# A conv-attention-scan network with a sorted mixture of experts: table numbers written earlier, two independent result adds, another spacing of expert tiles

## The chip, the cores and the metric

One Trainium2 chip, one of its cores. The metric is the device time of one execution in microseconds. The core has five engines with a queue each: TensorE (PE), VectorE (DVE), ScalarE (ACT), GpSimd (POOL) and SyncE (SP), which here only issues transfers. POOL and ACT issue transfers too[...].

## The reference, cut to what matters

```python
x = x + conv_block(_ln_c(x))          # 4 images of 256 channels, 32 x 32 points
t = _to_tokens(x)                     # 4 * 1024 tokens of 256
t = t + ffn(_ln_t(t))
def ffn(xf):                          # 8 experts, 2 of them for each token
    top_w, top_i = top_k(xf @ Wg + bg, 2);  top_w = softmax(top_w)
    for e in range(8):
        h = gelu(xf @ W1[e] + b1[e])  # 256 -> 1024
        out = out + w_dense[:, e:e+1] * (h @ W2[e] + b2[e])
```
`conv_block` is a layer norm, four selective scans of 64 channels each (state of 16), gates and short convolutions, attention with 8 heads beside a local convolution, a product of both with a norm and a gelu, a 3 x 3 convolution by channel, a norm and a last product.

## The kernel before

All of it is one program in float32. The Python code is a set of generators, each of which issues a part of the network and yields a number of ticks until it wants to be called again; `beat()` calls those whose tick has come. The order in which they are called is the order in each engine's queue, and nothing is moved afterwards.

**The front, by images.** The selective scan of an image has 4 x 2 parts of 16 steps. In a step ACT makes the decay `dA`, DVE the increment and the scan `hs` (lines 538, 545), POOL multiplies `hs` by the spread row `cs` (line 550), PE sums (line 556). Beside the scan of image b, `convolutions(b-1)`, `attention(b-1)`, `joined(b-1)`, `around(b-2)` and `sent_off(b-2)` run. `around` has the 3 x 3 taps on DVE: two chunks of channels, eight `scalar_tensor_tensor` each (line 1040). `sent_off` has the last norm (`mean`, squares `sq_fin`, `var_fin`, `r_fin`), the last product (`pr`) and `experts.dispatch`.

**Routing.** `dispatch(b)` turns the image into rows of tokens (transposes `raw`), stores them in `Y`, makes the gate's product, picks two experts for each token, and counts with two products `places` (lines 1499, 1500) where each row goes in a long array `XS` of one region per expert. `count` and `counted` are then known. It writes the rows with 16 indirect transfers from POOL (line 1560), a memset of a one-column tile `apart` ahead of each (line 1559), with a yield after each. At the last image, `blank_ends` first writes blank rows behind each region's end: ACT loads eight addresses from `ends_i` and issues eight transfers (line 1380).

**Tiles.** The expert part works on 39 tiles of 256 rows of one expert each: a first series of 8 after image 1 has been routed, a second of 8 after image 2, a third of 23 after image 3. `tiles()` issues 35 of them in order; the last 4 of the third series lie behind branches in `run` and are executed only if the number of tiles asks for them. A series starts with its table: `series` calls `tiles_of` and `table`, which write two number patterns with POOL's iota (`steps`, line 1582, and `which`, line 1603) and compute from them and the counts, in some 20 short DVE instructions, which expert and which row each tile has. `load` fetches a tile's weights, `rows` its 256 rows of `XS` (line 1709), both with an address that SP loads from the table. `front` transposes the rows (`xp`, line 1755, to `xT`, line 1756). `tile` makes the hidden rows (line 1778), gelu on ACT in pairs (line 1783), and the second product (line 1788); DVE adds a bias and weights the result `ys` (lines 1793, 1798), and two indirect transfers add it into `Y`, one for each half of 128 rows (line 1799). The second of them waits until the first has landed. A tile yields after each of its eight pieces, and while tile n is issued, `ahead(n + 1)` loads the next: its load in the first piece, rows in the second, front from the sixth on.

**Spacing.** After image 3's scan `convolutions(3)` is issued with `around(2)`, `sent_off(2)` and tiles, then `attention(3)` alone, then `joined(3)`, `around(3)`, `sent_off(3)` in one chain beside the tiles. In this chain `pace(b, ticks)` sets how many ticks a piece of a tile yields: the larger, the fewer pieces between two steps of the chain. The last tile of the second series is held until the rows of image 3 are sent.

At the end `bring_back` loads `Y` (line 1810), transposes it (line 1819) and stores it.

Of the kernel before, what the change touches and what calls it, by code (L numbers as in the profile page):

```python
# [9 lines left out]
F32 = mybir.dt.float32  # L10
# [4 lines left out]
P = 128  # L15
C = 256
# [6 lines left out]
NE, DFF = 8, 1024  # L23
# [48 lines left out]
def network(  # L72
# [70 lines left out]
    with tc.tile_pool(name="w_conv", bufs=1) as wp, tc.tile_pool(  # L143
# [902 lines left out]
        def sent_off(b):  # L1046

            xc = XC.pop(b)

            def centre(h, mean):  # L1050
                for c in range(NC2):
                    nc.vector.tensor_tensor(
                        xc[:, c, half(h)], xc[:, c, half(h)], mean, ALU.subtract
                    )

            pace(b, PACE["norm"])
            xr = a8(f"xr_{b}")
            nc.sync.dma_start(xr, x[b].rearrange("(c p) n -> p c n", p=P))
            yield from in_turn(
                range(2),  # L1060
                lambda h: column_mean(f"mean_{b}_{h}", [xc[:, c, half(h)] for c in range(NC2)]),
                centre,
            )
            yield from inverse_deviation(f"fin_{b}", xc)

            def residual(at, r):
                co, h = at
                inner = xr[:, co, half(h)]
                nc.vector.scalar_tensor_tensor(
                    inner, r, prb[:, co : co + 1], inner, ALU.add, ALU.add  # L1070
                )

            yield from in_turn(
                CO_H, lambda at: product(
                    f"pr_{b}_{at[0]}_{at[1]}", projT_s, at[0],
                    [xc[:, ci, half(at[1])] for ci in range(NC2)],
                ), residual,
            )
            pace(b, PACE["rows"])
            yield from experts.dispatch(  # L1080
                b, xr, act8.tile(experts.XR, F32, tag="a8", name=f"XR_{b}"), root,
                log_exp,
            )
            T["sent", b] = True
            pace(b, 1)


        def tiles():
# [3 lines left out]
            order = order[: len(order) - LATE]  # L1092
            got, xs, tables = {}, {}, experts.tables

            def known(n):
                return experts.counted >= B - 3 + order[n][0]

# [3 lines left out]
            def load(n):  # L1101
                s, i = order[n]
                if i == 0:
                    tables.append(experts.series(
                        s, lambda name, shape: act2.tile(shape, F32, tag="a2", name=name)
                    ))
                if n == 0:
                    w1 = [a8("w1_0")[:, :, 0:DFF]]
                    w2 = [a8("w2_0").rearrange("p c (k x) -> p (c k) x", x=C)]
                else:  # L1110
                    w = [
                        acts.tile([P, N], F32, tag="dts", name=f"w_{n}_{k}") for k in range(3)
                    ] + [actd.tile([P, N], F32, tag="dt", name=f"w_{n}_3")]
                    w1, w2 = w[0:2], [v.rearrange("p (k c) -> p k c", c=C) for v in w[2:4]]
                b2_s = actc.tile([P, C], F32, tag="cs", name=f"b2_{n}") if n else a2("b2_0")[:, 0:C]
                got[n] = experts.load(s, i, tables[s], w1, w2, b2_s)
# [22 lines left out]
            for n in range(len(order)):  # L1139
                while n not in got or len(got[n]) == 4:  # L1140
                    ahead(n, NHC)
                    yield 4

                while n == sum(experts.SERIES[:2]) - 1 and not sent(n + 1):
                    ahead(n + 1, 0)
                    yield 1
                while not T.get(("scanned",)):
                    yield 1
                while T.get(("hold",)):
# [58 lines left out]

        PARTS = 2 * NB

        PACE = {"product": 3, "norm": 1.7, "taps": 0.67, "rows": 1.6}
        with tc.manual_schedule(engines=ALL):
            log_exp()
            start(normalised(0), weights())
# [73 lines left out]
class Experts:  # L1288
# [7 lines left out]

    T = 256

    SERIES = (8, 8, 23)
# [4 lines left out]
    def __init__(self, ctx, tc, psum, B, b1, ident, eps5, ones_mean, Wg, bg, W1, W2, b2, out):  # L1306
# [10 lines left out]
            tc.tile_pool(name="moe_dram", bufs=1, space=bass.MemoryType.DRAM)  # L1317
        )
        self.XS = md.tile([self.SPARE + T, self.ROW], F32, name="XS")
        self.Y = md.tile([NTOK + P, C], F32, name="Y")  # L1320
        m0 = self.m0 = ctx.enter_context(tc.tile_pool(name="moe0", bufs=1))

        blank = self.blank = m0.tile([P, self.ROW], F32, name="blank")
        nc.gpsimd.memset(blank, 0.0)
        nc.gpsimd.iota(
            blank[:, C : C + 1], [[0, 1]], base=NTOK, channel_multiplier=1,
            allow_small_or_imprecise_dtypes=True,
        )
        nc.gpsimd.memset(blank[:, C + 3 : C + 4], -1.0)
        nc.scalar.dma_start(self.Y[ds(NTOK, P), :], blank[:, 0:C])  # L1330

        Wg_s = m0.tile([P, NC2, NE], F32, name="Wg_s")
        nc.gpsimd.dma_start(Wg_s, Wg)
# [38 lines left out]
        self.sent, self.sent_by = [], []  # L1372
        self.tables = []
        self.counted = -1
        self.read = []
        self.blank_rows(self.SPARE)

    def blank_rows(self, at):

        ins = self.nc.scalar.dma_start(  # L1380
            self.XS[ds(at, self.T), :].rearrange("(n p) c -> p n c", p=P),
            self.blank.rearrange("p (a c) -> p a c", a=1)
            .to_broadcast([P, self.T // P, self.ROW]),
        )
        for other in self.sent + self.read:
            self.tc.declare_no_dep(ins.ins, other.ins, reason="no two share a row")
        self.sent.append(ins)
# [47 lines left out]
    def dispatch(self, b, X1, XR, root, log_exp):  # L1435
# [117 lines left out]
        if b == self.B - 1:  # L1553
            self.blank_ends()

        apart = m0.tile([P, 1], F32, tag="apart", name=f"apart_{b}")
        for j in range(2):
            for t in range(NT):
                nc.gpsimd.memset(apart, 0.0)
# [15 lines left out]
        for other in others:  # L1575
            self.tc.add_manual_dep(ins.ins, other.ins.name, kind, reason=reason)

    def tiles_of(self, temp, name, rows, base=0):

        nc, K = self.nc, self.NTOK // self.T  # L1580
        steps = temp(f"steps_{name}", [P, NE, K])
        nc.gpsimd.iota(
            steps, [[0, NE], [self.T, K]], base=base, channel_multiplier=0,
            allow_small_or_imprecise_dtypes=True,
        )
        nc.vector.tensor_tensor(steps, rows.to_broadcast([P, NE, K]), steps, ALU.is_gt)
        ntile = temp(f"ntile_{name}", [P, 1, NE])
        nc.vector.tensor_reduce(ntile.rearrange("p a e -> p e a"), steps, AX.X, ALU.add)
        return ntile

    def table(self, temp, keep, name, n, ntile, done=None):


        nc = self.nc
# [4 lines left out]
        starts = temp(f"starts_{name}", [P, 1, NE])  # L1599
        nc.vector.tensor_tensor(starts, ends, ntile, ALU.subtract)  # L1600
        S = [P, n, NE]
        which, past = temp(f"which_{name}", S), temp(f"past_{name}", S)
        nc.gpsimd.iota(
            which, [[1, n], [0, NE]], base=0, channel_multiplier=0,
            allow_small_or_imprecise_dtypes=True,
        )
        nc.vector.tensor_tensor(past, which, ends.to_broadcast(S), ALU.is_ge)
        inside = temp(f"inside_{name}", S)
        nc.vector.tensor_tensor(inside, which, starts.to_broadcast(S), ALU.is_ge)
# [25 lines left out]
    def series(self, s, temp):  # L1635
# [7 lines left out]
            assert before + n == self.NTILE  # L1643
        else:
            assert (before + n) * T <= 2 * N * b - NE * (T - 1)
        ntile = self.tiles_of(temp, s, self.count[:, :, b : b + 1], 0 if last else T - 1)
        if s:
            nc.vector.tensor_tensor(ntile, ntile, self.done, ALU.subtract)
        table, starts, ends = self.table(temp, self.kept, s, n, ntile, self.done if s else None)
        if last:  # L1650
            self.used = self.m0.tile([P, 1], mybir.dt.int32, name="used")
            nc.vector.tensor_copy(self.used, ends[:, :, NE - 1 : NE].rearrange("p a e -> p (a e)"))
# [116 lines left out]
    def tile(self, j, got, hs, ys):  # L1769
# [26 lines left out]
        )  # L1796
        for t in range(2):
            nc.vector.tensor_scalar(ys[:, t, :], ys[:, t, :], wgt[:, t, :], None, ALU.mult)  # L1798
            nc.gpsimd.indirect_dma_start(  # L1799
                out=self.Y[:, :],  # L1800
                out_offset=bass.IndirectOffsetOnAxis(ap=dest[:, t, :], axis=0),
                in_=ys[:, t, :], in_offset=None, compute_op=ALU.add,
            )

    def bring_back(self, b, m2):

# [120 lines left out]
```

## Time and profile before

| | |
|---|---|
| time, median of 3 (lowest to highest) | 2480.68 us (2478.96 to 2487.04) |
| profiled execution: span, mean PE clock granted | 2485.2 us, 0.913 |
| busy, of the span: PE, DVE, ACT, POOL | 85%, 65%, 48%, 45% |
| scan of image 3 ends (last `hs` on POOL) | about 1684 us |
| attention of image 3 on PE | 1893 to 1964 us |
| `places` of image 3 | 2105.5 us |
| front of tile 16 | 2167.15 us |
| last product of the last tile ends | about 2444.5 us |

The profile's times run from the first instruction. A line of the timeline gives start, length, engine, line of the code, operation, what is written and read, and in brackets how long the engine stood idle before it and which instruction or transfer ended that. `SPq` and `ACTq` are the queues from which these engines issue transfers. One matrix product of the code makes two matmul records in float32. Ends of matmuls are modelled, and a few records can be missing.

### The profile page before, as it was taken

The page shows a single profiled execution, that of the slowest core. Times are in us where ns is not written, and L with a number is a line of the kernel's source. Part 1 is how long each engine was busy: PE and PEld are TensorE (multiplying, and loading weights), DVE is VectorE, ACT ScalarE, POOL GpSimd, SP SyncE. Part 2 cuts the span into 40 slices and gives each one's busy share as a digit, 9 for nine tenths or more (in the row PEclk, how much of TensorE's full clock was granted, in tenths as well). Part 3 has the DMA queues.
Part 4 walks back from the last instruction along what each step waited for, and adds up shares of the span by engine and source line. Part 5 has one row for each costly group of instructions (what it writes and reads, how often), then busy time and mean ns, then how long its engine had stood idle before and what let it go on. Part 6 is the DMA issues. An engine that isn't in the chain of part 4 may idle for free. (4 is left out here: it accounts for less than half of the span.)

```text
span 2485.2 us, 28288 instructions
## 1 busy us (share of the span) xinstructions
PE 2122.3 (85%) x8810; PEld 941.7 (38%) x8810; DVE 1622.3 (65%) x2243; ACT 1193.9 (48%) x2016; POOL 1111.8 (45%) x1163
## 2 busy tenths in 40 slices
PE   5776778899977799998589999758999999599995
PEld 2121112333311132232013223204773477588884
DVE  2688998876799887789978877985424354111211
ACT  1544455368663647765253686413427654122221
POOL 2577777541577661176775405562112011322221
PEclk8799997899998889997788999868999999899997
DMA  3443342220243321033333202334431154566664
GB/s 95 99 109 93 96 117 70 72 70 27 51 103 97 75 61 34 28 105 98 97 80 77 57 18 51 90 100 145 115 112 36 55 154 142 176 195 196 190 195 148
DMA packets 154541, 244.17 MB, mean 98 GB/s; under 512 B 34017, under 2 KB 103301, under 8 KB 154377
## 3 DMA queue, kind: packets, MB, share of 16 engines
q1 hardware_dynamic: 133856, 215.46, 30.7%
q0 software_dynamic: 13744, 19.31, 3.8%
q10 hardware_dynamic: 6776, 7.45, 0.9%
q8 instruction: 74, 1.21, 0.2%
q14 instruction: 91, 0.74, 0.1%
HBM read 141.16 MB, written 33.85 MB: 70 GB/s over the span
## 5 line engine op out<-in xcount | busy, mean ns | idle before, releaser
L550 POOL TENSOR_TENSOR hs<-hs,cs 128x512 f32<-128x512 f32 x512 | 669.5, 1309 | 222.0 <-DVE hs L545 175.1
L556 PE MATMUL yp<-hs,quads 128*32 128x512 f32 x1024 | 344.5, 684 | 173.1 <-POOL hs L550 123.2
L531 ACT ACTIVATE dA<-dts,A 128x512 f32<-128x512 f32 x512 | 342.9, 713 | 291.6 <-DMA dts<-dt 185.7
L538 DVE TENSOR_TENSOR dBu<-dts,bs 128x512 f32<-128x512 f32 x512 | 348.1, 680 | 80.5 <-DMA dts<-dt 24.2
L545 DVE TENSOR_TENSOR_SCAN hs<-dA,last,dBu 128x512 f32<-128x512 f32 x256 | 327.7, 1280 | 24.9 <-DVE dBu L538 0.5
L1799 POOL DMA_INDIRECT Y<-ys,dest x70 | 112.6, 1609 | 512.7 <-DVE ys L1798 362.2
L545 DVE TENSOR_TENSOR_SCAN hs<-dA,dBu 128x512 f32<-128x512 f32 x256 | 312.5, 1221 | 30.6 <-ACT dA L531 5.7
L1783 ACT ACTIVATE hs<-h,b 128x256 f32<-128x256 f32 x280 | 117.0, 471 | 405.5 <-PE h L1778 265.6
L871 ACT ACTIVATE e<-st 128x512 f32<-128x512 f32 x512 | 263.1, 606 | 87.2 <-PE st L861 86.7
L1788 PE MATMUL y<-w,hs 128*128 128x256 f32 x1120 | 259.6, 383 | 4.8 <-ACT hs L1783 4.8
L1778 PE MATMUL h<-xT,w 128*128 128x256 f32 x1120 | 253.2, 382 | 0.8 <-DVE xT L1756 0.8
L1788 PEld LDWEIGHTS y<-w,hs 128*128 128x128 f32 x1120 | 212.2, 192 | 43.4 <-issue 10.1
L1778 PEld LDWEIGHTS h<-xT,w 128*128 128x128 f32 x1120 | 213.3, 191 | 40.2 <-issue 9.7
L1756 DVE COPY xT<-xp 128x512 f32<-128x512 f32 x35 | 24.2, 692 | 297.8 <-PE xp L1755 297.8
L556 PEld LDWEIGHTS yp<-hs,quads 128*32 128x32 f32 x1024 | 55.6, 117 | 429.0 <-POOL hs L550 287.4
L523 PE MATMUL bs<-u,xpwT_s 128*32 128x512 f32 x1024 | 176.9, 670 | 40.6 <-DVE hs L545 23.6
L549 POOL COPY last<-hs 128x1 f32<-128x1 f32 x256 | 66.3, 259 | 318.0 <-DVE hs L545 309.5
L913 DVE TENSOR_TENSOR e<-e,e 128x512 f32<-128x512 f32 x256 | 171.4, 732 | 53.9 <-PE av L903 44.0
L861 PE MATMUL st<-qk 32*128 32x512 f32 x1024 | 194.0, 655 | 6.8 <-DVE hs L545 4.5
L439 PE MATMUL up<-xn,inwk 64*128 64x512 f32 x256 | 131.7, 659 | 15.6 <-DVE hs L545 9.2
L903 PE MATMUL av<-e,v 128*32 128x512 f32 x1024 | 142.7, 621 | 0.0
L861 PEld LDWEIGHTS st<-qk 32*128 32x128 f32 x1024 | 68.1, 188 | 132.4 <-issue 88.1
(271 smaller groups left out, 2499.3 us busy)
## 6 DMA issues: line engine op xcount, KB each, us to landing
w<-in_W_dram SPq DMA_DIRECT2D x136, 512.0 KB, 4.0
dts<-dt SPq DMA_DIRECT2D x512, 128.0 KB, 2.4
cs<-cd SPq DMA_DIRECT2D x512, 64.0 KB, 2.0
xs<-XS SPq DMA_DIRECT2D x35, 260.0 KB, 4.5
b<-in_b_dram SPq DMA_DIRECT2D x35, 128.0 KB, 4.2
xn<-in_x_dram SPq DMA_DIRECT2D x4, 1024.0 KB, 5.7
XL<-xl SPq DMA_DIRECT2D x8, 512.0 KB, 2.8
xl<-XL SPq DMA_DIRECT2D x4, 1024.0 KB
```

Source lines behind the costliest of these rows:

```text
L523: nc.tensor.matmul(bs[r], xpwT_s[:, n, s : s + 1].to_broadcast([P, 32]), T[b, n, "u"][:, half(h)], start=True, stop=True,)
L531: nc.scalar.activation(dA, T[b, n, h, "dts", g][:, 0, :], AF.Exp, scale=A[:, g, n, q : q + 1])
L538: nc.vector.tensor_tensor(dBu, T[b, n, h, "dts", g][:, 1, :], T[b, n, h, "bs", q], ALU.mult)
L545: nc.vector.tensor_tensor_scan(hs, T[b, n, h, "dA", i], dBu, 0.0 if h == 0 else last, ALU.mult, ALU.add)
L550: nc.gpsimd.tensor_tensor(hs, hs, T[b, n, h, "cs", q], ALU.mult)
L556: nc.tensor.matmul(T[b, n, h, "yp"][ts(g, 32)], quads, T[b, n, h, "hs", q * GD + g], start=(q == 0), stop=(q == GS - 1),)
L861: nc.tensor.matmul(sts[i], k[r, ts(kt, P)], q[r, half(h)], start=True, stop=not shifted)
L871: nc.scalar.activation(es[i], sts[i], AF.Exp, scale=1.0 / HD**0.5)
L903: nc.tensor.matmul(accs[0][ts(i, HD)], v8[:, kt, ts(4 * g + i, HD)], es[i], start=(kt == 0), stop=(kt == NK - 1),)
L913: nc.vector.tensor_tensor(first[i], first[i], es[i], ALU.add)
L1778: nc.tensor.matmul(hp[:, i, :], w1(c, k), xT[:, c, :], start=(c == 0), stop=(c == NC2 - 1))
L1788: nc.tensor.matmul(yp[:, ts(t, C)], hs[:, k, ts(t, P)], w2(k), start=(k == 0), stop=(k == NHC - 1))
```

## The change

1. **Number patterns.** A new function `count_up(s)` writes `steps` and `which` of series s. It is called for series 0 when `tiles()` starts, five ticks ahead of the rest, and for series 1 and 2 when tile 2 and tile 10 (the third of their series) start. `tiles_of` and `table` take the patterns instead of writing them.
2. **Adds.** The two adds of a tile are declared to be independent, with a memset of `apart` between them; each waits for both adds of the tile before. The rows of a blank tile get 256 different numbers instead of twice the same 128, for which `Y` and the tile `blank` grow. `apart` is one tile for the whole kernel.
3. **Spacing.** In the chain of image 3 a piece of a tile yields 4 ticks instead of 3 at the products, 2.2 instead of 1.7 at the norms, 0.9 instead of 0.67 at the taps, and in `dispatch` 2 until the counts are known and 0.75 after it instead of 1.6. The hold of the second series' last tile is removed.

```diff
-            pace(b, PACE["rows"])
-            yield from experts.dispatch(
+            pace(b, PACE["routing"])
+            for ticks in experts.dispatch(
                 b, xr, act8.tile(experts.XR, F32, tag="a8", name=f"XR_{b}"), root,
                 log_exp,
-            )
+            ):
+                if experts.counted == b:
+                    pace(b, PACE["rows"])
+                yield ticks
...
+            experts.count_up(0, temp)
+            yield 5
...
-                while n == sum(experts.SERIES[:2]) - 1 and not sent(n + 1):
-                    ahead(n + 1, 0)
-                    yield 1
+                if order[n] in ((0, 2), (1, 2)):
+                    experts.count_up(order[n][0] + 1, temp)
...
-        PACE = {"product": 3, "norm": 1.7, "taps": 0.67, "rows": 1.6}
+        PACE = {"product": 4, "norm": 2.2, "taps": 0.9, "routing": 2, "rows": 0.75}
...
-        self.Y = md.tile([NTOK + P, C], F32, name="Y")
+        self.Y = md.tile([NTOK + T, C], F32, name="Y")
...
+    def count_up(self, s, temp):
+        nc, K, n = self.nc, self.NTOK // self.T, self.SERIES[s]
+        steps = temp(f"steps_{s}", [P, NE, K])
+        nc.gpsimd.iota(steps, ...)
+        which = temp(f"which_{s}", [P, n, NE])
+        nc.gpsimd.iota(which, ...)
+        self.numbers[s] = steps, which
...
-            nc.gpsimd.indirect_dma_start(
+        added = []
+        for t in range(2):
+            if t:
+                nc.gpsimd.memset(self.apart, 0.0)
+            ins = nc.gpsimd.indirect_dma_start(
                 out=self.Y[:, :],
                 out_offset=bass.IndirectOffsetOnAxis(ap=dest[:, t, :], axis=0),
                 in_=ys[:, t, :], in_offset=None, compute_op=ALU.add,
             )
+            for other in added:
+                self.tc.declare_no_dep(ins.ins, other.ins, reason="no two share a row")
+            self.follow(ins, self.added, "a row may be added to by both")
+            added.append(ins)
+        self.added = added
```

## The prediction

> **What bounds the kernel now.** The chain of waits on the page starts at 2476.48 and says nothing here, so I read in this order: TensorE (PE) busy time by stage, who PE waits for, then the queue of each engine at the places found. All times are of the profiled execution (span 2485.2 us; the three timed runs gave 2478.96 to 2487.04, median 2480.68). I sum differences and put them on the median.
>
> Busy time by stage, from the end of image 3's attention (1964) on: length, busy us with record counts for PE, PE weight loads, DVE, ACT, POOL, then granted clock, DMA share, GB/s.
> ```profile
> 2001.00:2044.00 43.00, 40.32 (x187) 34.44 (x187) 30.88 (x44) 25.41 (x39) 9.82 (x5) 1.00 0.67 200
> 2044.00:2086.00 42.00, 37.05 (x145) 26.15 (x144) 13.06 (x28) 14.23 (x23) 6.19 (x4) 1.00 0.41 117
> 2086.00:2106.00 20.00, 19.93 (x119) 17.73 (x118) 10.74 (x44) 8.87 (x18) 3.10 (x2) 1.00 0.63 178
> 2106.00:2135.00 29.00, 26.17 (x126) 22.73 (x126) 10.17 (x42) 7.71 (x16) 14.76 (x23) 1.00 0.77 224
> 2135.00:2168.00 33.00, 10.60 (x50) 9.09 (x49) 5.31 (x22) 3.36 (x8) 11.23 (x17) 0.71 0.47 147
> 2168.00:2445.00 277.00, 276.62 (x1308) 242.84 (x1306) 48.68 (x153) 63.81 (x152) 58.61 (x38) 0.99 0.62 178
> ```
> Length minus PE busy is the idle: 2.7, 4.9, 0.1, 2.8, 22.4, 0.4 us. From 2168 PE is full and nothing but PE work counts; the 22.4 us is one wait. PE's waits from 1690 on (waiting line, releaser, total us, times, longest):
> ```profile
> PE xp L1755 <- DMA xs<-XS: 22.4, 1, 22.4
> PE op L1819 <- DMA yy<-Y: 19.6, 4, 16.2
> PE var_fin L343 <- ACT sq_fin L949: 6.5, 2, 3.7
> ```
> Tile 16, the first that needs the last routing, waits for its rows. Why so late is in POOL's queue (start, length, what, idle before it and its releaser):
> ```profile
> 1642.48 0.30 POOL L1582 IOTA steps<- 128x128 f32 x1
> ...
> 1649.13 1.27 POOL L550 TENSOR_TENSOR hs<-hs,cs 128x512 f32<-128x512 f32 x1 [6.18 <-DVE hs L545]
> ...
> 2144.04 1.61 POOL L1799 DMA_INDIRECT Y<-ys,dest  x1 [0.30 <-issue]
> 2148.62 1.56 POOL L1799 DMA_INDIRECT Y<-ys,dest  x1 [2.97 <-issue]
> 2149.63 0.86 POOL L1582 IOTA steps<- 128x128 f32 x1
> ```
> and in DVE's and ACT's:
> ```profile
> 2150.53 0.29 DVE L1586 TENSOR_TENSOR steps<-count,steps 128x128 f32<-128x128 f32 x1 [14.75 <-POOL steps L1582]
> ```
> ```profile
> 2115.94 10.27 ACTq L1380 DMA_DIRECT2D XS<-blank  x8
> 2126.26 3.03 ACT L1783 ACTIVATE hs<-h,b 128x256 f32<-128x256 f32 x8 [15.52 <-DMA XS<-blank]
> ```
> Line 1582 and line 1603 write the number patterns of a table. The third table's stood behind 16 row transfers and two scatter-adds; DVE idled 14.75 us for them. ACT could issue no gelu for 11.3 us (2114.99, end of ends_i, to 2126.26), held by eight address loads. The tail:
> ```profile
> 2445.90 1.54 POOL L1799 DMA_INDIRECT Y<-ys,dest  x1 [7.79 <-DVE ys L1798]
> 2450.47 1.54 POOL L1799 DMA_INDIRECT Y<-ys,dest  x1 [3.03 <-DMA Y<-ys,dest]
> 2455.74 8.32 SPq L1810 DMA_DIRECT2D yy<-Y  x8
> ```
>
> [...] idle from 2144.7, clock 0.57 in 2149 to 2150, 0.50 until work had run from 2167.15 to 2173. So a wait over 4.4 us costs 5.9 us at half speed: 3 us. [...] here the scatter-adds land 3.7 us or more after issue (median 5.0). [...]
>
> **The change, part by part.** A tile is 8 groups of 8 matmul records at 1.72 us each (7.07 us for 32 records).
>
> *Numbers ahead, first table.* POOL's order has the two iotas where they were (1642.48), but DVE's table work moves from right behind them to five scan steps later. Before, DVE waited 5.37 us for the iota and worked 4.15 us (1642.81 to 1646.96), and POOL, which sets the end of the scan here (it runs without a gap from 1649 to 1684), starved 6.18 us. Without the wait, 4.15 us stand against the slack of 9.5 - 6.18 = 3.3 us: POOL starves some 0.8 us. Bounds 3 and 6.2 saved; I take **-5 us**.
>
> *Numbers ahead, second table.* Its numbers are written at tile 2 and hold 2 of 17 act2 buffers through the attention. PE had no gap in the 71 us of attention and ACT was busy 59: nothing at best, 2 us at worst; I take 0.
>
> *Pace before the attention.* Image 2's product of squares meets its wait of 3.7 us (ACT sq_fin) one group earlier: **+1.7 us** (0 to 1.7).
>
> *Pace around the last routing.* By the instruction order, tile groups in front of each milestone, before and after: to the second var_lgn 7 and 6; to image 3's mean 22 and 16; to its first raw transpose 13 and 10; to places (L1499) 8 and 6. So 12 groups, 20.7 us of PE work, move behind the routing. What does the routing gain?
> - To var_lgn PE was full: -1.7.
> - To the mean: the chain is DVE's. Sixteen taps of 1.265 us (20.2 us) ran from 2019.7 to 2043.66, with 4.1 us of tile work between them; afterwards two xT and one ys, 4.5 us. ACT's order ahead of it (a gelu of 2.37, table loads of 1.28, hs pairs of 0.84) lets the first tap start 0.4 us sooner. Sum +0.3; six groups less only make PE idle 10.3 us more, over 7 us of it just ahead of the mean, so the mean meets half clock.
> - To raw: following ACT (hs pair, load, root 1.33, squares 1.14) and PE in the new order, the second var_fin waits some 4.8 us and the product 2.6; three groups less, half clock 3 us more: -1.8.
> - To places: two groups and a front less, DVE's choice of 5.4 us now the limit: -2.3.
> Together the routing comes **5.5 us earlier, not 20.7**.
>
> *After the routing.* From places to the end of tile 14's product there were 14 groups (28.7 us: 2105.5 to 2134.2) and are 26: 44.7 + three fronts of 0.44 + 0.5 = 46.5. But ACT now has only two hs pairs of tile 12 in front of the address loads. PE works 12.1 us without it (two groups, four, one, plus places); the loads end at ends_i (9 us after places) + 11.3 = 20.3. PE waits 8.1 us where it waited 2.8, and then runs at half clock: +3. That is 57.6, **+28.9 us**. POOL's 16 transfers (1.26 each) and the adds between end some 42 us after places, in time.
>
> *The third table.* It is emitted, as before, behind tile 14's ys in DVE's order. From there: ys 1.5 us, then what took 16.6 (2150.53 to 2167.15: table 4.8, weights and rows issued by 2160.64, landed, seen by PE) = 18.1 in place of 32.9: **-14.8**. PE has 10.4 us of work (tile 15 up to the front): a wait of 7.7 remains, and half clock behind it as before.
>
> *The removed hold* in front of the 16th tile adds no instruction; the new order has tile 15 at the same place. *A larger blank* (one memset, one store) lies in the start behind the weight loads: nothing.
>
> *Independent adds.* The adds wait for ys in every full-PE tile, no one waits for them, so nothing until the last. There the second starts after 1.54 + a memset of 0.1 + 0.2 instead of 4.57: **-2.7**, bounds -3 and -1 (two adds at once may land later). The new waits on both adds of the tile before are long served; behind them on POOL only row transfers queue.
>
> Sum: -5 + 1.7 + (-5.5 + 28.9 - 14.8 = 8.6) - 2.7 = +2.6 us. **Forecast 2483 us**, no change: what a measurement tells from no change here is about 0.3%, 7.4 us.
>
> **Rivals.**
> - *The routing comes much earlier* because DVE and ACT lose tile work too. For: 25.4 us of ACT and 30.9 of DVE in 43. Against: the taps alone are 20.2. If 15 us come instead of 5.5, the sum is -7 to -13 (the stages then wait less, too): 2469.
> - *The last wait goes altogether*: rows and weights of tile 16 are found ready. For: the issue of the weights needs only 5 us after the table. Against: the table is still behind ys. It saves 7.7 and 3: 2472.
> - *ACT's block grows* (slower): the eight loads take their 11.3 us in a stretch with DMA share 0.77; if transfers, weights and loads collide as PE stands still, 16 to 18 us instead, +6, and the clock drops twice more at waits near 4.8 us, +3. It decides as soon as the block ends over 12.1 us after places: 2492.
> - *The change doesn't do what it says*: were the second add still bound to the first, only 2.7 us would be missing: 2486, inside the forecast.
>
> **How the numbers follow.** Forecast 0.38 (its own range 2475 to 2490: same 0.27, faster 0.05, slower 0.06), early routing 0.25 (faster 0.22, same 0.03), no last wait 0.15 (faster 0.09, same 0.06), ACT's block 0.22 (slower 0.18, same 0.04). Faster 0.36, same 0.40, slower 0.24. The range for 8 in 10 reaches from inside the first rival to the third's time: 2465 to 2492.
>
> **What would show it.** Right: POOL's gap of 6.18 us near 1649 under 2; PE idle near 13 us in the taps; places 5 to 6 us nearer to the attention's end; a PE wait for ACT of about 8 us behind it with DMA XS<-blank as releaser; xp's wait 7 to 8 us; second add 1.9 us behind the first. Wrong: places over 10 us nearer, or no wait for ACT there, means faster; a wait for ACT over 12 us or longer attention means slower.

## The result, and the profile after

The changed kernel takes 2499.06 us (median of four, 2497.59 to 2500.28) against 2480.61 us (2478.96 to 2487.04) of the kernel before on the same chip: a ratio of 1.0069, 95% interval 1.0050 to 1.0088. It is **slower by 18.4 us**; the forecast was 2483 us and no change, and the range ended at 2492.

**Read two profiles from a common point.** The two profiled spans, 2485.2 and 2498.6 us, differ by 13.4 us only. POOL's row numbers of image 1 (the third last `IOTA XR`) stand ahead of the first table, and up to there both kernels issue the same instructions in the same order, but for the larger blank tile in the start. Yet they come at 1620.55 us in one execution and at 1616.96 in the other; over the kernels below this point lies anywhere from 1611 to 1628. The stretch from it to the attention's end repeats to some tenths (343.4 to 344.0 us in the kernels of the table below, e10's 341.8 apart). So I measure from it, by milestones of TensorE (PE), in us:

| stretch | before | after | difference |
|---|---|---|---|
| common point to end of image 3's attention | 343.7 | 344.0 | +0.3 |
| attention's end to `places` | 141.3 | 145.3 | +4.0 |
| `places` to front of tile 16 | 61.6 | 76.6 | +15.0 |
| front of tile 16 to last product of the tiles | 277.3 | 276.3 | -0.9 |
| tail | 40.8 | 39.4 | -1.4 |
| sum | 864.7 | 881.6 | +17.0 |

Between the attention's end and tile 16's front both kernels execute the same matmuls. Busy time by stage for these two stretches, first of the kernel before (columns: window, length, busy us with record counts for PE, PE weight loads, DVE, ACT, POOL, then granted clock, DMA share, GB/s):

```profile
1964.23:2105.53 141.30, 133.60 (x561) 99.73 (x560) 60.14 (x145) 64.34 (x107) 19.10 (x11) 1.00 0.49 147
2105.53:2167.15 61.62, 36.39 (x172) 31.44 (x172) 15.95 (x65) 11.54 (x25) 25.99 (x40) 0.85 0.61 182
```

and of the changed kernel:

```profile
1960.91:2106.21 145.30, 124.81 (x461) 88.05 (x461) 56.47 (x134) 58.53 (x95) 15.50 (x15) 0.90 0.38 115
2106.21:2182.85 76.64, 61.74 (x272) 53.24 (x273) 19.77 (x76) 14.79 (x34) 30.50 (x44) 0.90 0.66 198
```

561 + 172 and 461 + 272 are both 733 records. PE is idle for 7.7 + 25.2 = 32.9 us before and for 20.5 + 14.9 = 35.4 us after: 2.5 us more. But the same 733 records are busy for 170.0 us before and 186.6 us after: **16.6 us more for the same work**. The clock column tells why: in the first stretch it is 0.90 where it was 1.00. (The 0.85 of the second stretch before falls in the wait of 22.4 us, where PE has nothing to do.) Two clocks are granted here, 1.00 and 0.50, the half clock. Summed in steps of 1 us, PE's busy time times what is missing of the clock is 0.0 us before and 16.1 us after. The waits of PE in the changed kernel from 1690 on (line, releaser, total us, times, longest):

```profile
PE op L1847 <- DMA yy<-Y: 18.7, 5, 13.7
PE y L1806 <- ACT hs L1801: 11.8, 4, 7.5
PE var_fin L343 <- ACT sq_fin L949: 8.9, 3, 4.1
PE xp L1773 <- DMA xs<-XS: 7.4, 1, 7.4
PE mean L343 <- DVE xi L1040: 6.3, 2, 4.6
PE places L1508 <- DVE oh L1501: 3.3, 1, 3.3
PE var_lgn L343 <- ACT sq_lgn L949: 2.6, 1, 2.6
PE pr L334 <- DVE xi L961: 1.5, 1, 1.5
```

The one wait of 22.4 us is 7.4 now, and between the attention's end and tile 16's front eight of 1.2 to 7.5 us stand beside it, where the kernel before had four of 1.2 to 2.8. All of the eight but that at `pr` stand next to a stretch of half clock or in one. Stages of 2 us of the changed kernel, one amid the full work at 1968 and six behind waits or the gate's product:

```profile
1968.00:1970.00 2.00, 2.00 (x6) 0.80 (x6) 0.14 (x1) 1.97 (x5) 0.00 (x0) 1.00 0.57 168
1992.00:1994.00 2.00, 2.00 (x4) 0.79 (x3) 0.00 (x0) 0.98 (x1) 0.00 (x0) 0.57 0.04 14
2018.00:2020.00 2.00, 0.94 (x2) 0.83 (x3) 1.29 (x2) 1.37 (x3) 0.00 (x0) 0.50 0.00 0
2042.00:2044.00 2.00, 1.70 (x2) 0.84 (x3) 0.25 (x1) 0.00 (x0) 0.00 (x0) 0.50 0.00 0
2060.00:2062.00 2.00, 1.88 (x3) 0.96 (x4) 0.00 (x0) 1.86 (x3) 0.00 (x0) 0.63 0.00 0
2096.00:2098.00 2.00, 2.00 (x6) 1.64 (x7) 1.49 (x7) 0.00 (x0) 0.00 (x0) 0.50 1.00 392
2130.00:2132.00 2.00, 2.00 (x6) 1.55 (x6) 0.00 (x0) 0.22 (x1) 0.00 (x0) 0.50 0.83 252
```

The waits that precede four of them, in PE's timeline of the changed kernel (start, length, what, and in brackets the idle time before it with its releaser):

```profile
1991.22 2.78 PE L343 MATMUL var_lgn<-sq_lgn,ones_mean 128*128 128x512 f32 x4 [2.60 <-ACT sq_lgn L949]
2042.30 2.07 PE L343 MATMUL mean<-xi,ones_mean 128*128 128x512 f32 x2 [4.65 <-DVE xi L1040]
2060.12 3.40 PE L343 MATMUL var_fin<-sq_fin,ones_mean 128*128 128x512 f32 x4 [4.10 <-ACT sq_fin L949]
2129.18 3.48 PE L1806 MATMUL y<-w,hs 128*128 128x256 f32 x8 [7.47 <-ACT hs L1801]
```

Four records of `var_fin` take 3.40 us here; four of `mean` at full clock take 1.88. What the prediction was to be known by is half there. POOL's queue at the first table (line 1591 is the iota that was line 1582):

```profile
1638.94 0.30 POOL L1591 IOTA steps<- 128x128 f32 x1
...
1653.61 1.26 POOL L550 TENSOR_TENSOR hs<-hs,cs 128x512 f32<-128x512 f32 x1 [2.95 <-DVE hs L545]
```

The gap of 6.18 us is 2.95, where under 2 was named. PE's idle time in the taps is 9.0 us, where near 13 was named. ACT's block and the tail's adds:

```profile
2118.62 9.98 ACTq L1391 DMA_DIRECT2D XS<-blank  x8
2128.65 1.57 ACT L1801 ACTIVATE hs<-h,b 128x256 f32<-128x256 f32 x4 [11.24 <-DMA XS<-blank]
```

```profile
2460.65 1.54 POOL L1822 DMA_INDIRECT Y<-ys,dest  x1 [10.41 <-DVE ys L1816]
2461.63 0.68 POOL L1821 MEMSET apart<- 128x1 f32 x1
2462.50 1.56 POOL L1822 DMA_INDIRECT Y<-ys,dest  x1 [0.19 <-POOLq L1710]
```

The block is no longer than before (10.7 us from the end of `ends_i` at 2117.91, against 11.3), and the second add starts 1.85 us behind the first.

### The profile page after: what moved, and what is told of

Read it like the earlier page. It is cut to its first block, busy times and chain, and to the rows that moved or that the text cites. A ratio compares the mean times of both kernels' runs of the same rounds, so it can differ in the third digit from the quotient of the medians.

```text
span 2498.6 us, 28309 instructions
## 1 busy us (share of the span) xinstructions
PE 2132.0 (85%) x8810; PEld 948.7 (38%) x8810; DVE 1626.6 (65%) x2243; ACT 1190.0 (48%) x2014; POOL 1114.4 (45%) x1198
## 5 line engine op out<-in xcount | busy, mean ns | idle before, releaser
L545 DVE TENSOR_TENSOR_SCAN hs<-dA,dBu 128x512 f32<-128x512 f32 x256 | 312.4, 1220 | 31.6 <-ACT dA L531 6.8
L1806 PE MATMUL y<-w,hs 128*128 128x256 f32 x1120 | 269.2, 393 | 11.8 <-ACT hs L1801 11.8
L1806 PEld LDWEIGHTS y<-w,hs 128*128 128x128 f32 x1120 | 219.1, 198 | 54.6 <-ACT hs L1801 14.0
L1796 PEld LDWEIGHTS h<-xT,w 128*128 128x128 f32 x1120 | 214.0, 192 | 41.5 <-issue 10.7
L439 PE MATMUL up<-xn,inwk 64*128 64x512 f32 x256 | 135.1, 674 | 16.7 <-DVE hs L545 10.5
L903 PE MATMUL av<-e,v 128*32 128x512 f32 x1024 | 143.0, 623 | 0.0
```

What stands on the lines that cost most here:

```text
L545: nc.vector.tensor_tensor_scan(hs, T[b, n, h, "dA", i], dBu, 0.0 if h == 0 else last, ALU.mult, ALU.add)
L903: nc.tensor.matmul(accs[0][ts(i, HD)], v8[:, kt, ts(4 * g + i, HD)], es[i], start=(kt == 0), stop=(kt == NK - 1),)
L1796: nc.tensor.matmul(hp[:, i, :], w1(c, k), xT[:, c, :], start=(c == 0), stop=(c == NC2 - 1))
L1806: nc.tensor.matmul(yp[:, ts(t, C)], hs[:, k, ts(t, P)], w2(k), start=(k == 0), stop=(k == NHC - 1))
```

## The experiments

All times are set against the kernel before on the same chip. The stretches of the profiles together (e8 stands below), us, one profile of each kernel, with PE's idle time from the attention's end to tile 16's front ("idle"; the fillers of e5 and e10 count as work) and what half clock costs there ("cold"):

| kernel | ratio to before (95%) | to attention's end | to `places` | to front 16 | rest | idle | cold |
|---|---|---|---|---|---|---|---|
| before | 1 | 343.7 | 141.3 | 61.6 | 318.1 | 32.9 | 0.0 |
| changed | 1.0069 (1.0050 to 1.0088) | 344.0 | 145.3 | 76.6 | 315.8 | 35.4 | 16.1 |
| e1 old spacing | 0.9935 (0.9908 to 0.9961) | 343.7 | 141.3 | 51.3 | 313.3 | 22.3 | 0.0 |
| e2 spacing alone | 1.0095 (1.0065 to 1.0124) | 344.0 | 145.2 | 84.0 | 316.9 | 42.3 | 16.5 |
| e3 numbers alone | 0.9965 (0.9950 to 0.9980) | 344.0 | 142.7 | 54.4 | 318.3 | 19.6 | 7.7 |
| e4 adds alone | 0.9967 (0.9952 to 0.9981) | 343.9 | 141.3 | 55.8 | 316.0 | 26.9 | 0.0 |
| e5 fillers | 1.0036 (1.0017 to 1.0054) | 343.5 | 138.0 | 72.6 | 316.3 | 14.9 | 0.0 |
| e6 old spacing to the routing | 0.9925 (0.9897 to 0.9953) | 343.6 | 139.3 | 58.1 | 311.8 | 19.7 | 4.4 |
| e7 blanks on SyncE | 1.0042 (1.0024 to 1.0060) | 343.4 | 145.5 | 72.8 | 315.6 | 31.6 | 16.3 |
| e9 e1, table early | 0.9911 (0.9876 to 0.9946) | 343.7 | 142.8 | 42.6 | 312.3 | 12.3 | 3.3 |
| e10 filled wait | 1.0006 (0.9997 to 1.0016) | 341.8 | 143.0 | 67.1 | 314.3 | 14.5 | 5.1 |
| e11 old spacing at the taps | 0.9967 (0.9953 to 0.9981) | 343.9 | 139.4 | 62.8 | 314.7 | 22.0 | 10.2 |
| e12 picks together | 1.0063 (1.0044 to 1.0082) | 343.5 | 142.0 | 76.6 | 314.3 | 34.4 | 14.0 |

### One part at a time

Theory A: the spacing costs, numbers and adds gain. Theory B: the spacing is neutral and one of the others costs.

**e1.** The changed kernel with the old spacing and the hold:

```diff
-        PACE = {"product": 4, "norm": 2.2, "taps": 0.9, "routing": 2, "rows": 0.75}
+        PACE = {"product": 3, "norm": 1.7, "taps": 0.67, "rows": 1.6}
...
```

> The changed kernel with the spacing of before (3, 1.7, 0.67, 1.6, and the hold of the 16th tile); numbers written ahead and independent adds stay. Theory A (the spacing costs, the other two parts gain): the third table no longer stands behind the row transfers, so DVE's 14.75 us of waiting goes and tile 16's front waits 7.7 us in place of 22.4; with 3.3 us from the first table and 2.7 us at the tail the sum is -21: about 2460 us. Theory B (the spacing is neutral, the numbers or the adds cost, by the two act2 buffers held through the attention or by adds that collide with the row transfers): it stays where the changed kernel is, 2495 to 2500 us.

2469.86 us, ratio 0.9935. Theory B falls. The wait of tile 16 is 11.2 us, not 7.7, and the first table gives nothing, so the gain in the profile, 15.1 us from the common point on, is smaller than A's 21.

**e2.** The kernel before with the new `PACE`, its switch in `sent_off`, and without the hold:

```diff
-        PACE = {"product": 3, "norm": 1.7, "taps": 0.67, "rows": 1.6}
+        PACE = {"product": 4, "norm": 2.2, "taps": 0.9, "routing": 2, "rows": 0.75}
...
```

> The kernel before with the new spacing alone (and without the hold). Theory A: the routing's counting product comes no earlier than before and 12 groups of tile work stand behind it; the table waits for POOL's numbers behind four pairs of adds and 16 row transfers besides, some 6.7 us later than in the changed kernel; with the 3.3 us of the first table and the 2.7 us of the tail missing as well: about 2511 us. Theory B: 2480 to 2485 us.

2505.90 us, ratio 1.0095. The two stretches in question are those of the changed kernel but for the later table (15.2 us of wait for tile 16's rows in place of 7.4), with the same 16 us of cold.

**e3.** The kernel before with `count_up`, called where the change calls it:

```diff
+            experts.count_up(0, temp)
+            yield 5
...
+                if order[n] in ((0, 2), (1, 2)):
+                    experts.count_up(order[n][0] + 1, temp)
```

> The kernel before with the number patterns ahead alone. Theory A: tile 16's rows now wait for the last row transfer (issued to 2143.7, landed some 3 us later) and its weights for a table that starts at 2135.8: front at about 2153 in place of 2167, -14; and -3.3 from the first table: about 2463 us. Theory B: 2480 us or slower if the two held buffers cost.

2476.69 us, ratio 0.9965: half of what A expected. Tile 16's wait falls from 22.4 to 4.9 us, but PE's waits for ACT's `hs` grow from 4.8 to 9.0 us, and 7.7 us of cold appear where there were none. And the first table's gain is not there. The scan of image 3 ends 3.2 us earlier (60.5 in place of 63.7 us behind the common point), the attention at the same time. In between, these waits of PE in e3 are new or longer (start behind the common point 94.5 and 126.9 us): 1.65 us for DVE's `xi` at image 2's mean and 1.14 us for ACT's `sq_fin` at image 2's second `var_fin`, 2.8 of the 3.2 us.

**e4.** The kernel before with the independent adds:

```diff
+            for other in added:
+                self.tc.declare_no_dep(ins.ins, other.ins, reason="no two share a row")
+            self.follow(ins, self.added, "a row may be added to by both")
...
```

> The kernel before with the independent adds alone. Theory A: the second add of tile 13 no longer holds POOL for 6.92 us with twelve row transfers behind it, and that of tile 14 no longer for 2.97, so the numbers of the third table are written at about 2140.5 in place of 2149.6; -9 there and -2.7 at the tail: about 2469 us. Prediction's view (adds are nothing until the last tile): -2.7, 2478 us.

2477.11 us, ratio 0.9967: times 2480.61 us this is 2472 us (2469 to 2476), with A's 2469 at the edge and 2478 outside. The profile agrees: tile 16's wait is 15.1 us instead of 22.4, its front comes 5.8 us earlier behind `places`, and the tail is 1.6 us shorter. So the adds are worth some 6 us in the middle of the kernel, if the table's numbers stand behind them in POOL's queue; the prediction held them for nothing there.

### Is it the clock?

**e5.** The changed kernel with products of a constant at the places where PE waits, written into the PSUM tile of the next product:

```diff
             out = ps(name)
+            for _ in range(FILL.get(name, 0)):
+                nc.tensor.matmul(out[:, 0:P], ones_mean, experts.every, start=True, stop=True)
...
```

> The changed kernel with filler products (128 columns of a constant, into a part of the same PSUM tile that the real product overwrites or leaves alone) where TensorE waits between the end of the attention and tile 15: 10 ahead of the first var_lgn, 18 ahead of the first mean, 17 ahead of the second var_fin, 8 among the gate's, 12 ahead of places, 18 and 30 ahead of the second products of tiles 8 and 12; 113 of about 0.22 us, 25 us against 26 us of waits. Half-clock theory (the 16.6 us that the same matmuls take longer than in the kernel before are the price of the waits): they come back but for the gate's fillers (1.8 us): 2485 us or less. Rival (the waits themselves and the longer chain cost, the clock is not on the path): 2499 to 2504 us.

2495.61 us, ratio 1.0036 against the changed kernel's 1.0069, and 11.3 us less from the common point on (870.4 against 881.6). Times 2480.61 us the ratio gives 2490 us (2485 to 2494): the rival's 2499 falls, and the 2485 of the half-clock theory is only just reached. Twelve fillers write `places` ahead of the real product, so this milestone is taken behind them, at 2109.22. Busy time by stage of e5:

```profile
1971.24:2109.22 137.98, 131.42 (x626) 99.83 (x626) 56.36 (x134) 58.56 (x95) 15.38 (x15) 1.00 0.41 122
2109.22:2181.84 72.62, 64.26 (x333) 56.79 (x333) 19.78 (x76) 14.79 (x34) 30.51 (x44) 0.97 0.73 204
```

The clock is full wherever PE works (0.0 us of cold). Although 25 us of work were added, `places` comes 7.3 us earlier than in the changed kernel, with 11.9 us of cold ahead of it gone, and tile 16's front 11.3 us earlier, with 16.1 gone. Nothing is removed from the chain: the order of all real instructions is that of the changed kernel. So the half clock is on the path, and it is paid for by the waits. It is not all of the loss: by the profile e5 is still 5.7 us slower than the kernel before. Some 1.8 us of fillers stand between the gate's products, where PE doesn't wait; and 30 of them, 6.9 us, in front of tile 12's second product leave a wait of 1.0 us there.

**e10.** The same from the other side: the kernel before with 90 fillers in the wait of 22.4 us.

```diff
         xp = psum.tile([P, HALF], F32, tag="ps", name=f"xp_{j}")
+        for _ in range(90 if j == 16 else 0):
+            nc.tensor.matmul(xp[:, 0:P], self.ident, self.every, start=True, stop=True)
```

> The kernel before with 90 filler products of about 0.22 us (20 us) in TensorE's wait of 22.4 us ahead of tile 16's front, into the same PSUM tile, overwritten by the front. If the clock is granted by what TensorE has just done and not by the change, the 2.95 us that the 15 us behind that wait lose to half clock go: the stretch from places to the last product 2 to 3 us shorter, the time 2478 to 2480 us. If the clock is set otherwise: the stretch is as long as before or longer.

2484.56 us, ratio 1.0006 (0.9997 to 1.0016). Of the clock the first view holds. The ten us behind the wait in e10:

```profile
2165.06:2175.06 10.00, 10.00 (x51) 8.86 (x50) 2.54 (x8) 2.40 (x6) 1.56 (x1) 1.00 0.59 152
```

The 15 us behind the front lose 0.0 us to half clock, where the kernel before loses 2.95, and from the front to the last product of the tiles there are 274.4 us in place of 277.3. The whole time doesn't show it: from `places` to the last product it is 2.5 us more, as the second view had it, because the front came 5.4 us later. The fillers ran on to it (2165.06 us), and from the attention's end on PE waited 6.8 us for ACT's `hs` in place of 4.8 and lost 5.1 us to half clock in three other stretches.

**When the clock falls.** In each of the fourteen profiles all changes of the granted clock, 2065 together, lie on a grid of 3.413 us, and PE's busy time within one interval of the grid goes with the clock of the next. From the attention's end to tile 16's front, the intervals with the gate's products apart, full clock was kept behind each of 678 intervals in which PE was busy for 1.50 us or more, and lost behind each of 49 with 1.47 us or less. It came back behind intervals with 2.90 us or more. (From the common point on, 170 falls and 2877 without have an overlap, between 1.41 and 1.57 us.) So in this stretch some 1.9 us of idle time in one interval (3.413 less 1.47 to 1.50) went with a fall, and it matters how a wait lies across the grid. The wait of 2.60 us at `var_lgn`, with the two intervals that it touches and the one behind them, first in the changed kernel, then in e8, an experiment that is described further down:

```profile
1985.44:1988.86 3.41, 3.17 (x12) 1.90 (x10) 0.00 (x0) 0.20 (x1) 0.00 (x0) 1.00 0.00 0
1988.86:1992.27 3.41, 1.05 (x3) 0.58 (x4) 0.00 (x0) 3.40 (x7) 0.00 (x0) 1.00 0.82 307
1992.27:1995.68 3.41, 3.41 (x8) 2.03 (x7) 0.00 (x0) 2.33 (x4) 0.00 (x0) 0.50 0.00 0
```

```profile
2007.06:2010.47 3.41, 2.48 (x10) 1.52 (x8) 0.00 (x0) 0.89 (x3) 0.00 (x0) 1.00 0.11 29
2010.47:2013.89 3.41, 1.74 (x4) 0.87 (x5) 0.00 (x0) 3.40 (x5) 0.00 (x0) 1.00 0.71 278
2013.89:2017.30 3.41, 3.41 (x17) 2.94 (x16) 0.00 (x0) 2.38 (x5) 0.00 (x0) 1.00 0.00 0
```

In the first, 2.36 us of the wait lie in one interval, and the clock falls; in the second the wait is split into 0.93 and 1.67 us, and it doesn't. So a part of each kernel's cold is its place on the grid: behind the gate e3 and e9 lose 1.7 us that the kernel before, with the same products in the same order, does not. In twelve of the fourteen profiles the attention ends 0.73 to 0.89 of an interval behind an edge of the grid (e8 0.61, e10 0.30); what the changed order would cost at other places was not measured.

### Which spacing, and what else stands in the chain

**e6.** The changed kernel with the old spacing at products, norms and taps only:

```diff
-        PACE = {"product": 4, "norm": 2.2, "taps": 0.9, "routing": 2, "rows": 0.75}
+        PACE = {"product": 3, "norm": 1.7, "taps": 0.67, "routing": 2, "rows": 0.75}
```

> The changed kernel with the spacing of before at the products, norms and taps (3, 1.7, 0.67) and the new one in the routing (2, then 0.75). If the few pieces between the attention and the routing cost, nearly all comes back: the stretch to the first raw transpose is as in the kernel before, two groups less stand in front of places, 16 behind it, and tile 16's front is bound by the table: 2468 to 2472 us, the 2470 of the old spacing altogether. If the spacing in the routing costs (ACT's block by the blank rows' address loads, the row transfers spread between tiles): 2485 us or more.

2468.76 us, ratio 0.9925: all of the loss is gone. The spacing inside the routing costs nothing that can be measured.

**e11.** At the taps only:

```diff
-        PACE = {"product": 4, "norm": 2.2, "taps": 0.9, "routing": 2, "rows": 0.75}
+        PACE = {"product": 4, "norm": 2.2, "taps": 0.67, "routing": 2, "rows": 0.75}
```

> The changed kernel with the taps' spacing of before alone (0.67 for 0.9): 27 groups of tile work in place of 23 ahead of the mean, 30 in the kernel before. If the taps' wait and the wait for tile 8's hs ahead of it are the main loss, the half-clock stretches at 55 to 62 and 79 to 86 us behind the attention go, 7 us, with 3 us of waits: about 2489 us. If the loss is spread over all the waits of the chain: 2495 us or more.

2476.91 us, ratio 0.9967, and 20.8 us less than the changed kernel from the common point on: more than expected. Four groups of tile work, 6.9 us of PE time, are back in front of image 3's mean, and the last group of mean products starts at 86.9 us behind the attention with them and at 86.3 without: **they were nearly free there**. DVE's sixteen taps end 2.8 us later with them (84.2 in place of 81.3 us), but the changed kernel loses 2.3 us to half clock around the mean, and e11 nothing. The rest is the chain behind it: the waits of 4.65 us at the mean, 4.10 at `var_fin` and 1.49 at `pr` shrink to 0.6, 0 and 0, the first `raw` comes at 115.2 in place of 122.3 us, and ACT's block meets PE with a wait of 1.9 us in place of 7.5.

**e7.** ACT's block: the changed kernel with the blank rows' loads and transfers in SyncE's queue.

```diff
-        ins = self.nc.scalar.dma_start(
+        ins = (engine or self.nc.scalar).dma_start(
...
-                    ends[0:1, e, :], engines=[mybir.EngineType.Activation], min_val=0,
+                    ends[0:1, e, :], engines=[mybir.EngineType.SP], min_val=0,
```

> The changed kernel with the eight blank-row transfers and their address loads on SyncE's queue instead of ScalarE's. If ACT's block costs what it shows: TensorE's wait of 7.47 us for hs goes and 3 us of half clock behind it: 2489 us. If the wait only moves (the table's weights then stand behind the eight loads in SyncE's queue, or the routing's rows set the time of tile 16 anyway): 2496 to 2502 us.

2497.09 us, ratio 1.0042, an interval that overlaps that of the changed kernel; by the profile the stretch behind `places` is 3.8 us shorter, not 10. The wait for ACT behind `places` goes, but half of it moves. In e7's queues:

```profile
2114.72 8.76 SPq L1391 DMA_DIRECT2D XS<-blank  x8
...
2128.89 0.38 SPq L1728 DMA_DIRECT2D xs<-XS  x1
```

```profile
2137.42 0.66 PE L1774 MATMUL xp<-ident,xs 128*128 128x128 f32 x4 [3.40 <-DMA xs<-XS]
```

The weights and rows of a tile now stand behind the eight transfers, and that tile's front waits 3.40 us.

**e8 and e12.** DVE's queue in the changed kernel between the gate and `places`:

```profile
2098.05 0.22 DVE L1432 TENSOR_TENSOR eq<-num,at 128x64 f32<-128x64 f32 x1
2102.91 0.69 DVE L1774 COPY xT<-xp 128x512 f32<-128x512 f32 x1 [4.63 <-PE xp L1773]
...
2104.12 0.22 DVE L1496 SCALAR_TENSOR_TENSOR lg<-eq,lg 128x64 f32<-128x64 f32 x1
```

DVE has its first pick at 2098.3, and the copy of tile 12's front, for which PE is not ready until it has done 16 records of tile work at half clock, stands in front of the second pick. e8 and e12 take away the yield between the picks:

```diff
         m_1, oh1, at1 = self.first_largest(lg, "1")
-        yield 1
```

> The changed kernel without the yield between DVE's first and second pick of an expert, so that no tile's front (the copy xT, 4.63 us idle ahead of it) can stand between them in DVE's queue. If that interleaving is what makes places late: the wait of 3.34 us ahead of places goes and places comes that much earlier, 2493 to 2496 us. If PE's half clock between gate and places sets it: within 1 us of the changed kernel.

> The changed kernel without the yield between DVE's first and second pick, for image 3 alone, so that TensorE's order stays as it is and on DVE only tile 12's front moves behind the second pick. If that front (DVE idle 4.63 us ahead of it, for a product that TensorE reaches after 6.4 us of half-clock work) makes places late: places stands 3 to 4 us nearer to the attention's end than 145.3, TensorE's wait of 3.3 us there goes, and the time is 2492 to 2496 us. If TensorE's half clock between gate and places sets it alone: 145 us, and the changed kernel's time.

e8 took it away for every image, which changed the order ahead of image 3's attention as well; that ended 24 us later: 2501.64 us, ratio 1.0068 (1.0044 to 1.0093), and no answer, so it is not in the table. e12 takes it away for image 3 alone. `places` comes at 142.0 instead of 145.3 us: the expected 3.3. But the stretch behind it is as long as before, 76.6 us: PE comes to ACT's block earlier and waits 9.95 us there in place of 7.47, and the clock is down from 16 to 26 us behind `places`. From the common point on it is 5.2 us faster, 1.5 of them in the tail; the times (2498.88 us, ratio 1.0063) do not resolve it.

**e9.** A version from what was seen: e1 with the third table's DVE instructions right behind `ends_i`, instead of behind tile 14's result.

```diff
-                if i == 0:
+                if len(tables) <= s:
                     tables.append(experts.series(s, temp))
...
+                    if len(tables) == 2 and experts.ended:
+                        tables.append(experts.series(2, temp))
                     ahead(n + 1, at)
```

> The kernel of e1 (old spacing, numbers ahead, independent adds) with the third table's DVE instructions issued right behind those of ends_i, no longer behind the result of tile 14. If that place in DVE's queue sets what remains of tile 16's wait (11.2 us in e1), weights are asked for as soon as tile 14 frees its buffers, about 2136 in place of 2145: the wait falls to 3 or 4 us and with it 1.5 us of half clock: about 2461 us. If the row transfers or the weights' buffers set it: 2468 to 2471 us.

2457.93 us, ratio 0.9911 (0.9876 to 0.9946): faster than both kernels. e9's table is ready at 2113.8 us, and its front waits

```profile
PE xp L1777 <- DMA xs<-XS: 1.4, 1, 1.4
```

where e1's waited 11.2; this is the one long wait that both kernels had left.

## Why the prediction was wrong, point by point

**The first table (-5 us): wrong.** The gap went from 6.18 to 2.95 us, not to 0.8, and the 3.2 us at the scan's end did not reach the end of the attention. I had looked only at what sets the end of the scan, not at who is next: image 2's taps on DVE and squares on ACT were not earlier, and PE waited for them. **Image 2's `var_fin` (+1.7)** was put down to the spacing; with the spacing alone (e2) that wait is 3.7 us as before, and the new one comes with the numbers (e3). Both terms together: -3.3 predicted, +0.3 measured, 3.6 us of the error. The **second table (0)** fits with that: the attention, which runs on PE from 1876.4 us in the kernel before and so is 88 us long, not 71, shows no gap there and ends at the same time.

**The way to `places` (-5.5 us): the step that failed.** It came 4.0 us later, 9.5 us of the error. By its own parts, each counted from the attention's end: to the last `var_lgn` -1.7 predicted, +2.8 measured; to the last mean -1.4 and +3.8; to `raw` -3.2 and +0.8; to `places` -5.5 and +4.0. The working had three half-clock stretches (behind the mean, behind `var_fin`, behind the wait for ACT) because it let the clock fall only behind waits of over 4.4 us. That figure was an estimate, read from one wait: PE stopped at 2144.7, the interval of the grid began at 2145.7, and the clock fell at its end, 2149.1. Up to tile 16's front there are seven stretches, of 1.5 to 3.4 us, which sum to 16.1, 11.9 of them ahead of `places`. Four were not in the working: behind 2.60 us at `var_lgn`, a wait that the working didn't have either (1.7 us), at tile 8's second product (2.8), behind the gate (3.4) and at the wait for `places` (2.8). With the clock kept up (e5) the first `raw` comes 4.9 us earlier than in the kernel before and `places` 3.3 us: the chain of DVE and ACT had been read nearly right as far as `raw`, and **the size of the cold term was what was missed**, 7.3 us by e5. Of the last part, gate to `places`, 3.3 us are another thing that I had not seen: a tile's front between DVE's two picks (e12). "DVE's choice now the limit" took the choice for one block. No run took both away together.

**From `places` to the end of tile 14's product (57.6 us, +28.9): right in its sum**, 58.7 us, and in part by luck. The wait for ACT was predicted as 8.1 us and is 7.47, with the releaser named; but PE reaches it 15.5 us behind `places`, not 12.1, and ACT's block ends at 22.4, not 20.3. Half clock costs 4.3 us there in place of 3, and only 1.5 of them stand behind this wait, 2.8 behind the one at `places`. e7 shows that it is real, and that half of it would come back from SyncE's queue.

**The third table (-14.8 us, a wait of 7.7 left): right.** From tile 14's end to the front of tile 16 it is 17.96 us against 18.1, and the wait is 7.44. e9 shows that its place behind tile 14's result is what was left to gain.

**The adds (-2.7): right in the place, wrong in its reason.** From the last product to the issue of the first load of `Y` there are 8.58 us in place of 11.31, -2.73; the tail as a whole is 1.4 us shorter, as the last group of `op` then starts 20.30 us behind that issue in place of 19.56, and the end comes 10.5 us behind its start in place of 9.9. "Nothing until the last" is true only because the numbers no longer stand behind the adds (e4).

Of the **rivals**, the slower one had the right kind of price and the wrong place: ACT's block did not grow (10.7 us), and the clock drops that it counted as 3 us lay for the most part in the chain ahead of it, 11.9 of 16.1 us. The early routing failed since the chain did not get shorter by losing tile work; the last wait stayed.

Together: 3.6 (to the attention's end) + 9.5 (to `places`) + 0.9 (to tile 16's front, +14.1 predicted) - 0.9 (the tiles from there on) + 1.3 (the tail) are the 14.4 us between the predicted +2.6 and the +17.0 of the profiles. The work taken out of the chain was nearly free there: without 12 groups or 20.7 us of PE work `places` came 3.3 us earlier even with the clock kept up (e5), and the four groups that e11 put back in front of the mean cost 0.6 us where they were.

## What to carry to other kernels

Work that fills the waits of a chain on another engine is free until the chain gets longer by it (in e11 6.9 us of it cost 0.6 us ahead of the mean); before you take it out, find out which engine sets the chain's time in each stretch, and price the wait that you open with the half clock behind it, also where the wait is short (1.7 us behind the 2.60 us at `var_lgn` of the changed kernel). An estimate for this kernel, from the grid of 3.413 us and the 1.47 to 1.50 us above: with full work around it a wait of under 1.9 us costs no clock, one of over twice as much, 3.8 us, does, and between them it depends on where the wait falls. An instruction is freed by moving what it waits for only if its place in the queue is moved too (tile 16's wait: 11.2 us in e1, 1.4 in e9), and the gain is kept only if the next work on the path is ready earlier as well (the 3.2 us that e3 gained at the scan's end were gone at the attention's end). Compare two profiles from the last point up to which they issue the same instructions.

## What the runs showed of the hardware that was not expected

- **Short waits cost the clock.** In each profile the clock changes on a grid of 3.413 us, and an interval did not have to be idle as a whole for the clock to fall behind it: from the attention's end to tile 16's front, the gate's products apart, it fell behind 49 of 49 intervals with PE busy for 1.47 us or less (some 1.9 us of idle time or more) and behind none of the 678 with 1.50 or more. So 1.95 us cost the clock in e10, where they lay in one interval, and 2.78 us did not in the kernel before, where they lay 1.39 and 1.39 in two.
- **The clock fell behind narrow products as well.** Behind the gate's 32 records of 8 columns, with PE recorded as busy throughout, it fell in the nine profiles that have 2.32 us or more of them in one interval, and not in the four that have 2.23 or less (e5, with fillers between them, apart).
- **A stretch at half clock costs 1.5 to 3.4 us in the changed kernel**, and fillers that lie in waits give most of it back: up to tile 16's front, 11.3 of 16.1 us (e5).
- **The same instructions take up to 17 us more or less** over the first 1611 to 1628 us of an execution, while the stretch behind them up to the attention's end is 343.4 to 344.0 us in the kernels of the table. In e10 it is 341.8: there a wait of 3.71 us at image 2's `var_fin` is not followed by half clock, as it is in the others. What makes the first part vary is not shown.
